# A two-layer graph network: the order of the adjacency's columns, scaling in place, x loads nine ahead in halves, and h turned before a weight

## The chip, the cores and the metric

The kernel runs on one core of a Trainium2 chip. The metric is device time in microseconds (us); that of the kernel before is the median of three runs. A core has five engines with an instruction stream each: TensorE (PE in the profile; its weight loads are PEld), VectorE (DVE), ScalarE (ACT), GpSimd (POOL) and SyncE (SP). Here SP and POOL issue the transfers (DMA). SBUF is the memory on the chip, of 128 partitions; PSUM is the one TensorE writes to; DRAM is outside.

## The reference

There are B = 16 batches of N = 1024 nodes with C = 256 channels, all in fp32. Cut to what matters:

```
# layer 0
h  = max(layernorm(x), 0)
m  = mean over channels of h                      # one number for each node
A  = |  |sigmoid(m_j - m_i) - 0.5| - 0.5 | * 2 ;  A_s = (A + A^T)/2
q  = relu((h^T @ (adj * A_s)) * para)^T           # "graph"
k, v = split(h @ kv_w)
x  = x + softmax(q k^T * scale) v                 # 4 heads of 64 channels
# layer 1
h  = max(layernorm(x), 0)
A_n   = adj + I
deg   = column sums of A_n + row sums of A_n - diagonal of A_n ;  dinv = 1/sqrt(deg)
A_hat = A_n * dinv[:, None] * dinv[None, :]
z1 = (A_hat @ h) @ W1^T + b1                      # 512 channels
z2 = relu(batchnorm(z1)) @ W2^T + b2              # 256 channels
x  = x + batchnorm(z2)
```

The two batch norms take their statistics over all batches and nodes, so the second layer can't be finished batch by batch: everything up to z1 must be there for all batches before z2 begins, and all of z2 before the end.

## The kernel before, in words

The work is written into one function, `fast_path`, with the orders of all engines written by hand (`tc.manual_schedule`): an engine runs its instructions in the order of the program text and waits where an operand isn't ready. Tile pools decide which buffer a new tile gets; a tile whose buffer is still in use waits for the last reader.

**Start.** `turn_adj` (L688) turns adj through TensorE into `ahatT`, eight groups of 128 nodes, copied out of PSUM by ACT (four) and VectorE (four) at L692. `diagonal` (L707) picks the diagonal and adds the identity on POOL, 16 instructions at L711 and L712, and VectorE sums what was picked (L713). `column_sums`, `roots`, `roots_row` (L725 copies a row out of PSUM) and `scale_adj` (L728) make A_hat out of it; the last two are laid between the matmuls of batch 1's graph. The columns of `ahatT` are the nodes in their own order.

**Stage 1, batch by batch.** For batch b the loop runs the attention of b (scores L362, exponentials on ACT, values L403), then the graph of b+1, and then linear1 of b (A_hat @ h at L551, W1 at L624; out of PSUM by L635 on VectorE and L637 on ACT), which stores z1 to DRAM; the x of layer 1 goes to DRAM too. The graph (L291) takes 64 matmuls L308, eight steps c of eight, over the weights w of c = 0 to 7. Each w is made by ACT in two instructions (L262, L265) and finished by VectorE (L266). Then follow k (L326) and v (L341), which need h with the channels on partitions. That is what `turn_h` (L271) makes: two VectorE transposes of 32x32 blocks (L278), one for each half of the channels, and 32 transfers of 32 KB (L285) on POOL's queue that put the blocks in their place (`f_hT<-f_hQ`). What stands between the matmuls of a graph is given by the dict `between` (L796): ahead of c = 0 stand w of c = 2 (`more(2)`), `turn_h`, the steps `left` of the attention that is ending, w of 3 and of 4. TensorE has no part in these steps; VectorE, ACT and POOL run them in this order.

**Stage 2.** The 32 blocks of 512 columns of z1 come back from DRAM (pool `io`, AHEAD = 7 buffers of 1 MB; `Pair.load`, `fetch_all` at L1025), batch norm and relu are applied, and z2 = W2 @ relu(...) is computed, mostly in pairs of blocks (`Pair`); z2 stays in SBUF but for the last batch, which stays in PSUM. After the last pair the first seven x of layer 1 are requested on SP (L1082, `load_x1` at L871, 1 MB in each transfer with 8 KB in a row). The last products (L1119) of four z tiles, which lie in four buffers "z" of the pool `lasting`, close the statistics.

**The end** (L1148) runs over the batches. The output's rows are dealt so that partition p holds nodes 8p to 8p+7, "(p i)". `finish` scales z2 of the next batch with the batch norm's factors, ACT the first half of the channels (L1138), VectorE the second (L1140); it reads z2 with a step of 8 elements, so that the nodes p*8+i of one i become neighbours, and writes tiles `f_zo` in the four "z" buffers. TensorE turns them, 16 transposes in each batch (L1158), into two PSUM buffers; VectorE adds each half to x (L1167); POOL stores each half, 512 KB (L1168); and SP then requests the x of batch b+7, which waits for the stores of batch b, whose buffer it takes:

```
for i0, ps in zip(range(0, NC, 4), outs):
    here = xt[:, i0 : i0 + 4, :]
    nc.vector.tensor_add(here, here, ps)
    nc.gpsimd.dma_start(out_v[:, i0 : i0 + 4, :], here)
if b + AHEAD < B:
    load_x1(b + AHEAD)
```

Of the kernel before, what the change touches and what calls it, by code (L numbers as in the profile page):

```python
# [17 lines left out]
P = 128  # L18
# [3 lines left out]

ENG = mybir.EngineType
I32 = mybir.dt.int32
AHEAD = 7
LIMIT = 1e18


# [1 line left out]
def fast_path(  # L30
# [124 lines left out]
    with ExitStack() as stage:  # L155
# [522 lines left out]
                xs[b] = load_x(b)  # L678


        ahatT = big.tile([P, NC, N], F32, tag="ahatT", name="f_ahatT")
        deg = small.tile([P, NC], F32, tag="deg", name="f_deg", bufs=1)
        rsum = small.tile([P, NC], F32, tag="rsum", name="f_rsum", bufs=1)
        diag = small.tile([P, NC], F32, tag="diag", name="f_diag", bufs=1)
# [3 lines left out]
        def turn_adj(i, copy):  # L688
            ps = ps_s.tile([P, NC, P], F32, tag="s", name=f"f_adjps_{i}")
            for m in range(NC):  # L690
                nc.tensor.transpose(ps[:, m, :], adj_t[i][:, ts(m, P)], ident)
            copy(ahatT[:, :, ts(i, P)], ps)  # L692

        def unused(name):
            return pp.tile([P, N], F32, tag="p", name=f"f_unused_{name}")
# [11 lines left out]
        def diagonal():  # L707
            on = unused("d").rearrange("p (m q) -> p m q", q=P)
            for m in range(NC):
                block = ahatT[:, m, ts(m, P)]  # L710
                nc.gpsimd.tensor_mul(on[:, m, :], block, ident)  # L711
                nc.gpsimd.tensor_add(block, block, ident)  # L712
            nc.vector.tensor_reduce(diag, on, AX.X, ALU.add)  # L713

        def roots():
# [25 lines left out]
        with tc.manual_schedule(engines={ENG.PE, ENG.Activation, ENG.DVE, ENG.Pool, ENG.SP}):  # L741
# [35 lines left out]
            for b in range(B):  # L777
# [14 lines left out]
                def more(c):  # L792
# [71 lines left out]

    with ExitStack() as stage:
        big = stage.enter_context(tc.tile_pool(name="fbig2", bufs=1))
        io = stage.enter_context(tc.tile_pool(name="fio", bufs=AHEAD))

        xts = {}

        def load_x1(b):  # L871

            xts[b] = io.tile([P, NC, C], F32, tag="x1", name=f"f_x1t_{b}")
            nc.sync.dma_start(xts[b], x1_d[b].rearrange("(p i) d -> p i d", i=NC))

        st2 = big.tile([P, CC, TT, 6], F32, tag="st2", name="f_st2")
        with tc.manual_schedule(engines={ENG.PE, ENG.Activation, ENG.DVE, ENG.Pool, ENG.SP}):
# [39 lines left out]
            class Pair:  # L917
# [5 lines left out]
                def load(self):  # L923
                    p = self.p
                    t0, t1 = self.t

                    def two(name):
                        t = io.tile([P, 2, 2, 512], F32, tag="x1", name=f"f_z{name}_{p}")
                        return t[:, 0], t[:, 1]

                    self.t2, self.t3 = two("t23")
                    one, other = two("b1")
                    self.b[0, 0] = fetch(t0, 0, one)
                    self.b[1, 0] = fetch(t0, 2)
                    self.b[0, 1] = fetch(t1, 0, other)
                    one, self.t4 = two("b2")
                    self.b[1, 1] = fetch(t1, 2, one)

                def relu(self, k, j):
                    relu_on(self.b[k, j], 2 * k)  # L940
# [114 lines left out]
            for p in SEVEN:  # L1055
                now, soon = pairs[p], pairs.get(p + 1)
                if p + 2 in pairs:
                    pairs[p + 2].load()
                now.m2()
                stats(now.t[0], 0)  # L1060
                if soon:
                    soon.relu(0, 0)
                    soon.relu(0, 1)
                now.m6()
                now.keep(0, 1)
                now.m7()
                if soon:
                    soon.relu(1, 1)
                    soon.relu(1, 0)
                now.m5()  # L1070
                now.keep(1, 1)
                if soon:
                    soon.sums13()
                    soon.m1()
                    soon.keep(0, 0)
                else:
                    for t in rest:
                        fetch_all(t)
# [43 lines left out]
                bn2.invert(c, c + 1)  # L1122
                bn2.affine(c, c + 1)


            turned_z = {}

            def finish(b, c, i0, i1):
                if i0 == 0:
                    turned_z[b, c] = lasting.tile(  # L1130
                        [P, NC, P], F32, tag="z", name=f"f_zo_{b}_{c}", bufs=4
                    )

                def scaled(out, src):
                    src = src.rearrange("p (q i) -> p i q", i=NC)[:, i0:i1, :]
                    s, t = bn2.s[:, c : c + 1], bn2.t[:, c : c + 1]
                    if c == 0:
                        nc.scalar.activation(out, src, AF.Identity, bias=t, scale=s)  # L1138
                    else:
                        nc.vector.tensor_scalar(out, src, s, t, ALU.mult, ALU.add)  # L1140

                if b + 1 < B:
                    scaled(turned_z[b, c][:, i0:i1, :], z2[:, c, b, :])
                else:
                    for g in range(NH):
                        scaled(turned_z[b, c][:, i0:i1, ts(g, P // NH)], last[g, c])

            for b in range(B):  # L1148
                xt = xts.pop(b)
# [2 lines left out]
                for i0 in range(0, NC, 4):  # L1152
                    ps = ps_out.tile([P, 4, C], F32, tag="out", name=f"f_outps_{b}_{i0}")
                    for c in range(CC):
                        if b == 0:
                            finish(b, c, i0, i0 + 4)
                        for i in range(4):
                            nc.tensor.transpose(  # L1158
                                ps[:, i, ts(c, P)], turned_z[b, c][:, i0 + i, :], ident
                            )  # L1160
                    outs.append(ps)
                if b + 1 < B:
                    for c in range(CC):
                        finish(b + 1, c, 0, NC)
                for i0, ps in zip(range(0, NC, 4), outs):
                    here = xt[:, i0 : i0 + 4, :]
                    nc.vector.tensor_add(here, here, ps)  # L1167
                    nc.gpsimd.dma_start(out_v[:, i0 : i0 + 4, :], here)  # L1168
                if b + AHEAD < B:
# [515 lines left out]
```

## Time and profile before

| | |
|---|---|
| median of three runs | 2504.25 us (2500.96 to 2507.36) |
| profiled execution | 2502.86 us, of it the span 2501.1; mean clock of TensorE 0.992 |
| moved by DMA | 263.42 MB, 105 GB/s over the span |
| DMA packets | 169239; under 2 KB 120465, under 8 KB 166545 |
| x loads of the end, f_x1t<-fx | 16 of 1 MB, 8.2 us from issue to landing (median) |
| stores of the end, out_dram<-f_x1t | 32 of 512 KB, 13.2 us |
| hT transfers, L285 | 480 on POOL (and 32 for the first batch on SP) |

The span is one execution on the chip, taken by the profiler; the table of times holds other executions of the same program, which differ by up to 0.26% from one another. A row of the profile's groups reads: line, engine, operation, result<-operands by the program's names, partitions x elements, number; busy us in all and mean ns of one; and then the idle time of that engine just ahead of these instructions, with what ended most of it. In the 40 slices a digit is the busy share in tenths. The list of waits names for each wait of an engine the instruction or transfer that ended it.

### The profile page before, as it was taken

The page shows a single profiled execution, that of the slowest core. Times are in us where ns is not written, and L with a number is a line of the kernel's source. Part 1 is how long each engine was busy: PE and PEld are TensorE (multiplying, and loading weights), DVE is VectorE, ACT ScalarE, POOL GpSimd, SP SyncE. Part 2 cuts the span into 40 slices and gives each one's busy share as a digit, 9 for nine tenths or more (in the row PEclk, how much of TensorE's full clock was granted, in tenths as well). Part 3 has the DMA queues.
Part 4 walks back from the last instruction along what each step waited for, and adds up shares of the span by engine and source line. Part 5 has one row for each costly group of instructions (what it writes and reads, how often), then busy time and mean ns, then how long its engine had stood idle before and what let it go on. Part 6 is the DMA issues. An engine that isn't in the chain of part 4 may idle for free.

```text
span 2501.1 us, 24402 instructions
## 1 busy us (share of the span) xinstructions
PE 2432.2 (97%) x8122; PEld 1074.5 (43%) x8122; DVE 1625.7 (65%) x2223; ACT 1302.0 (52%) x1854; POOL 328.1 (13%) x577
## 2 busy tenths in 40 slices
PE   7999999999999999999999999999999999999984
PEld 4443444434343434344443434343444434444443
DVE  4786667484838475665848393857667586567665
ACT  7845545454636464554536363645555456256543
POOL 2030202020110302020202002030202020000012
PEclk9999999999999999999999999999999999999997
DMA  5031414131322324141322232242424120445549
GB/s 168 7 129 59 135 59 135 59 104 53 107 84 63 115 62 132 59 135 59 118 70 87 71 94 91 59 127 59 135 60 135 59 68 29 148 172 180 212 159 355
DMA packets 169239, 263.42 MB, mean 105 GB/s; under 512 B 37009, under 2 KB 120465, under 8 KB 166545
## 3 DMA queue, kind: packets, MB, share of 16 engines
q1 hardware_dynamic: 148944, 229.23, 28.4%
q0 software_dynamic: 20160, 32.55, 4.1%
q8 instruction: 66, 1.08, 0.2%
q14 instruction: 69, 0.56, 0.1%
HBM read 157.82 MB, written 70.31 MB: 91 GB/s over the span
## 4 chain that ended last, share of the span: by engine, by line
PE 82%; DMA 7%; DVE 5%; ACT 3%; issue 1%; SPq 1%; POOL 1%; DVEq 0%; POOLq 0%; ACTq 0%
PE f_s L362 15%; PE f_o L403 15%; PE f_aps L551 15%; PE f_gps L308 13%; PE f_zps L624 8%; PE f_vps L341 4%; PE f_kps L326 4%; PE f_zx L953 3%; PE f_zm L953 2%; DMA out_dram<-f_x1t 2%; PE f_z2ps L889 2%; DVE f_acc L379 1%; DMA f_hT<-f_hQ 1%; SPq L467 1%; DMA frow<-f_sums 1%
## 5 line engine op out<-in xcount | busy, mean ns | idle before, releaser
L370 ACT ACTIVATE f_p<-f_s 128x1024 f32<-128x1024 f32 x512 | 477.3, 1046 | 145.4 <-PE f_s L362 144.0
L379 DVE TENSOR_TENSOR f_acc<-f_acc,f_p 128x1024 f32<-128x1024 f32 x384 | 470.5, 1225 | 41.1 <-DVE f_acc L379 1.4
L362 PE MATMUL f_s<-f_qT,f_kT 64*128 64x512 f32 x2048 | 458.1, 596 | 0.0
L403 PE MATMUL f_o<-f_p,f_v 128*64 128x512 f32 x2048 | 453.6, 595 | 0.0
L308 PE MATMUL f_gps<-f_w,f_h_a 128*128 128x512 f32 x1024 | 444.7, 594 | 2.2 <-DVE f_w L266 2.2
L285 POOL DMA_DIRECT2D f_hT<-f_hQ x480 | 235.7, 499 | 1226.0 <-DVE f_hQ L278 838.3
L362 PEld LDWEIGHTS f_s<-f_qT,f_kT 64*128 64x128 f32 x2048 | 189.4, 185 | 265.9 <-ACT f_p L370 121.6
L308 PEld LDWEIGHTS f_gps<-f_w,f_h_a 128*128 128x128 f32 x1024 | 192.8, 190 | 250.4 <-issue 229.3
L403 PEld LDWEIGHTS f_o<-f_p,f_v 128*64 128x64 f32 x2048 | 141.4, 137 | 304.3 <-issue 274.0
L624 PE MATMUL f_zps<-f_aggT,f_w1T 128*128 128x512 f32 x512 | 222.5, 592 | 0.0
L266 DVE SCALAR_TENSOR_TENSOR f_w<-f_w,f_adj 128x1024 f32<-128x1024 f32 x128 | 155.1, 1213 | 83.2 <-ACT f_w L265 76.2
L262 ACT ACTIVATE f_w<-f_row,f_col 128x1024 f32<-128x1024 f32 x128 | 148.2, 1158 | 52.3 <-DMA f_row<-frow 47.7
L637 ACT ACTIVATE f_z<-f_zps,f_b 128x512 f32<-128x512 f32 x98 | 62.1, 684 | 202.9 <-PE f_zps L624 202.9
L219 ACT ACTIVATE f_h_a<-f_x,f_shift_a,f_rstd_a 128x256 f32<-128x256 f32 x128 | 75.0, 587 | 175.5 <-DVE f_shift_a L214 175.5
L641 DVE BATCH_NORM_STATS2 f_st<-f_z 128x6 f32<-128x512 f32 x128 | 82.2, 684 | 124.6 <-ACT f_z L637 124.6
L219 ACT ACTIVATE f_h_b<-f_x,f_shift_b,f_rstd_b 128x256 f32<-128x256 f32 x128 | 64.6, 587 | 170.7 <-DVE f_shift_b L214 170.7
L624 PEld LDWEIGHTS f_zps<-f_aggT,f_w1T 128*128 128x128 f32 x512 | 97.2, 190 | 122.0 <-issue 122.0
L265 ACT ACTIVATE f_w<-f_w 128x1024 f32<-128x1024 f32 x128 | 135.3, 1057 | 4.1
L593 DVE TENSOR_TENSOR f_aggT<-f_u,f_aps 128x512 f32<-128x512 f32 x16 | 11.0, 688 | 180.5 <-PE f_aps L551 180.5
L326 PE MATMUL f_kps<-f_hT,f_kvw 128*128 128x512 f32 x256 | 114.6, 595 | 6.4 <-DMA f_hT<-f_hQ 5.5
L551 PE MATMUL f_aps<-f_ahatT,f_hs 128*128 128x512 f32 x256 | 115.1, 592 | 0.0
L551 PE MATMUL f_aps<-f_ahatT,f_h_b 128*128 128x512 f32 x256 | 112.9, 593 | 0.9 <-ACT f_z L637 0.9
(151 smaller groups left out, 2453.5 us busy)
## 6 DMA issues: line engine op xcount, KB each, us to landing
f_t<-ft SPq DMA_DIRECT2D x84, 512.0 KB, 8.2
f_x<-in_x_dram SPq DMA_DIRECT2D x32, 1024.0 KB, 6.0
fz<-f_z SPq DMA_DIRECT2D x64, 512.0 KB, 3.5
f_zb<-fz SPq DMA_DIRECT2D x36, 512.0 KB, 4.5
f_para<-in_L_gnn_para_dram SPq DMA_DIRECT2D x32, 512.0 KB, 4.7
f_att<-f_oT SPq DMA_DIRECT2D x512, 32.0 KB, 1.9
fx<-f_x SPq DMA_DIRECT2D x16, 1024.0 KB, 6.0
f_x1t<-fx SPq DMA_DIRECT2D x16, 1024.0 KB, 8.2
```

The source lines that it names most:

```text
L219: nc.scalar.activation(self.h[:, c, :], self.xt[:, c, :], AF.Relu, bias=self.shift[:, c : c + 1], scale=self.rstd[:, c : c + 1], accum_out ...
L262: nc.scalar.activation(w, rows[b], AF.Abs, bias=cols[b][:, c : c + 1], scale=0.5 / C)
L266: nc.vector.scalar_tensor_tensor(w, w, 1.0, adj_t[c], ALU.subtract, ALU.mult)
L285: queue.dma_start(to[ts(k, 32), ts(a, 32 * NC)], t[ts(a, 32), k].rearrange("i c r -> i (c r)"),)
L308: nc.tensor.matmul(gps[d][:, ts(g, 512)], hs[b][:, c, ts(d, P)], w[:, ts(g, 512)], start=(c == 0), stop=(c == NC - 1),)
L326: nc.tensor.matmul(ps[:, ts(g, 512)], kvw_t[:, e, ts(d, P)], hT[e][:, ts(g, 512)], start=(e == 0), stop=(e == CC - 1),)
L362: nc.tensor.matmul(ps[:, e, :], kT[rows_e, pair, ts(m, P)], qT[rows_e, pair, ts(g, 512)], start=True, stop=True,)
L370: nc.scalar.activation(p, ps, AF.Exp)
L379: nc.vector.tensor_add(acc_of[s], acc_of[s], p)
L403: nc.tensor.matmul(o_of[s][e * HD : (e + 1) * HD, :], v[:, m, ts(2 * pair + e, HD)], p[:, e, :], start=(m == 0), stop=(m == NC - 1),)
L551: nc.tensor.matmul(ps, left[:, m, :], right(m), start=(m == 0), stop=(m == KH - 1),)
L624: nc.tensor.matmul(ps[:, i, :], w1T[:, d, ts(f, P)], aggT[:, d, :], start=(d == 0), stop=(d == CC - 1),)
```

## The change

Four edits go together.

1. The columns of `ahatT` are put in the end's order: column i*128+p holds node 8p+i. `turn_adj`'s copies write runs of 16 and read PSUM at a step of 8, `diagonal`'s POOL operations go over views with a step of 8, and the row of factors is copied in the same order. So z1 and z2 come out in this order too.
2. In the end `finish` scales in place in z2, contiguously, and writes no `f_zo`; the last batch goes from PSUM into the buffers of `w2n` and `w2T`. The transposes read z2.
3. AHEAD is 9. The pool `io` holds 14 half buffers (512 KB) in place of 7 whole ones, and every load of x for the end comes as two halves of 4 KB in a row. Seven batches are requested as before; two more, 7 and 8, are requested after the last statistics' instructions in the program's text, into the four "z" buffers, which no `f_zo` needs any more. In the end batches 9 to 15 are requested, each into the half buffers of batches 0 to 6. z1's blocks of `fetch_all` come as two halves of 512 KB.
4. In `between[0]`, `turn_h(b + 1)` stands ahead of `more(2)`.

```diff
-AHEAD = 7
+AHEAD = 9
...
+        ROW = P // NC
+        def columns(i):
+            view = ahatT.rearrange("p m (i q) -> p m i q", i=NC)
+            return view[:, :, :, ROW * i : ROW * (i + 1)]
+        def as_columns(nodes):
+            return nodes.rearrange("p (q i) -> p i q", i=NC)
...
-            copy(ahatT[:, :, ts(i, P)], ps)
+            copy(columns(i), ps.rearrange("p m (q i) -> p m i q", i=NC))
...
-                block = ahatT[:, m, ts(m, P)]
-                nc.gpsimd.tensor_mul(on[:, m, :], block, ident)
-                nc.gpsimd.tensor_add(block, block, ident)
+                block = columns(m)[:, m]
+                nc.gpsimd.tensor_mul(as_columns(on[:, m, :]), block, as_columns(ident))
+                nc.gpsimd.tensor_add(block, block, as_columns(ident))
...
-            nc.scalar.copy(t, ps.rearrange("p c q -> p (c q)"))
+            nc.scalar.copy(
+                t.rearrange("p (i c q) -> p c i q", i=NC, c=NC),
+                ps.rearrange("p c (q i) -> p c i q", i=NC),
+            )
...
-                        more(2), lambda: turn_h(b + 1), left[0], left[1], left[2], more(3),
+                        lambda: turn_h(b + 1), more(2), left[0], left[1], left[2], more(3),
...
-        io = stage.enter_context(tc.tile_pool(name="fio", bufs=AHEAD))
+        io = stage.enter_context(tc.tile_pool(name="fio", bufs=NH * (AHEAD - 2)))
...
-        def load_x1(b):
-
-            xts[b] = io.tile([P, NC, C], F32, tag="x1", name=f"f_x1t_{b}")
-            nc.sync.dma_start(xts[b], x1_d[b].rearrange("(p i) d -> p i d", i=NC))
+        def load_x1(b, pool=None, tag="x1", bufs=None):
+
+            xts[b] = []
+            for h in range(NH):
+                t = (pool or io).tile([P, NC // NH, C], F32, tag=tag, name=f"f_x1t_{b}_{h}", bufs=bufs)
+                nc.sync.dma_start(t, x1_d[b].rearrange("(p h i) d -> p h i d", h=NH, p=P)[:, h])
+                xts[b].append(t)
...
-                z = io.tile([P, FC, 512], F32, tag="x1", name=f"f_zz_{t}")
-                nc.sync.dma_start(z, z1_d[t])
                 for f2 in range(0, FC, 2):
-                    zs[t, f2] = z[:, f2 : f2 + 2, :]
+                    z = io.tile([P, 2, 512], F32, tag="x1", name=f"f_zz_{t}_{f2}")
+                    zs[t, f2] = fetch(t, f2, z)
...
-                    for n in range(AHEAD):
+                    for n in range(AHEAD - 2):
                         load_x1(n)
...
+            for b in range(AHEAD - 2, AHEAD):
+                load_x1(b, lasting, "z", 4)
+            ready = {}
             def finish(b, c, i0, i1):
-                if i0 == 0:
-                    turned_z[b, c] = lasting.tile(
-                        [P, NC, P], F32, tag="z", name=f"f_zo_{b}_{c}", bufs=4
-                    )
+                s, t = bn2.s[:, c : c + 1], bn2.t[:, c : c + 1]
                 def scaled(out, src):
-                    src = src.rearrange("p (q i) -> p i q", i=NC)[:, i0:i1, :]
-                    s, t = bn2.s[:, c : c + 1], bn2.t[:, c : c + 1]
                     if c == 0:
                         nc.scalar.activation(out, src, AF.Identity, bias=t, scale=s)
                     else:
                         nc.vector.tensor_scalar(out, src, s, t, ALU.mult, ALU.add)
                 if b + 1 < B:
-                    scaled(turned_z[b, c][:, i0:i1, :], z2[:, c, b, :])
+                    ready[b, c] = z2[:, c, b, :]
+                    at = ready[b, c][:, i0 * P : i1 * P]
+                    scaled(at, at)
                 else:
+                    ready[b, c] = lasting.tile(
+                        [P, N], F32, tag=("w2n", "w2T")[c], name=f"f_zo_{c}"
+                    )
                     for g in range(NH):
-                        scaled(turned_z[b, c][:, i0:i1, ts(g, P // NH)], last[g, c])
+                        scaled(ready[b, c][:, ts(g, 512)], last[g, c])
...
-                                ps[:, i, ts(c, P)], turned_z[b, c][:, i0 + i, :], ident
+                                ps[:, i, ts(c, P)], ready[b, c][:, ts(i0 + i, P)], ident
...
-                    here = xt[:, i0 : i0 + 4, :]
+                    here = xt[i0 // 4]
```

`Pair.load` takes its buffers as half buffers too, at the same places.

More of the change, by code (lines that the diff above doesn't have):

```diff
@@ L925, in load, with new @@
                     t0, t1 = self.t
[L927 to L933, printed above, removed]
+                    def new(name):
+                        return io.tile([P, 2, 512], F32, tag="x1", name=f"f_z{name}_{p}")
+                    self.t2, self.t3 = new("t2"), new("t3")
+                    self.b[0, 0] = fetch(t0, 0, new("b11"))
                     self.b[1, 0] = fetch(t0, 2)
-                    self.b[0, 1] = fetch(t1, 0, other)
-                    one, self.t4 = two("b2")
-                    self.b[1, 1] = fetch(t1, 2, one)
+                    self.b[0, 1] = fetch(t1, 0, new("b12"))
+                    self.b[1, 1] = fetch(t1, 2, new("b22"))
+                    self.t4 = new("t4")
                 def relu(self, k, j):
@@ L1123, in fast_path @@
                 bn2.affine(c, c + 1)
-            turned_z = {}
+            for b in range(AHEAD - 2, AHEAD):
+                load_x1(b, lasting, "z", 4)
+            ready = {}
             def finish(b, c, i0, i1):
-                if i0 == 0:
-                    turned_z[b, c] = lasting.tile(
-                        [P, NC, P], F32, tag="z", name=f"f_zo_{b}_{c}", bufs=4
-                    )
+                s, t = bn2.s[:, c : c + 1], bn2.t[:, c : c + 1]
                 def scaled(out, src):
-                    src = src.rearrange("p (q i) -> p i q", i=NC)[:, i0:i1, :]
-                    s, t = bn2.s[:, c : c + 1], bn2.t[:, c : c + 1]
                     if c == 0:
```

## The prediction, made before the changed kernel ran

> **What bounds the kernel now.** I read the page's busy shares first, then the slices, TensorE's waits, and at last the end by windows and timeline.
>
> ```profile
> PE 2432.2 (97%) x8122; PEld 1074.5 (43%) x8122; DVE 1625.7 (65%) x2223; ACT 1302.0 (52%) x1854; POOL 328.1 (13%) x577
> PE   7999999999999999999999999999999999999984
> DMA  5031414131322324141322232242424120445549
> PE 82%; DMA 7%; DVE 5%; ACT 3%; issue 1%; SPq 1%; POOL 1%; DVEq 0%; POOLq 0%; ACTq 0%
> ```
>
> TensorE is busy 97% of the span, and 9 tenths in every slice but the first and the last two. The change removes no matmul, so all it can win is in TensorE's waits and in the two ends of the span. The waits:
>
> ```profile
> PE f_outps L1158 <- DVE f_x1t L1167: 21.2, 14, 4.3
> PE f_adjps L691 <- DMA f_adj<-in_adj_dram: 8.5, 1, 8.5
> PE f_kps L326 <- DMA f_hT<-f_hQ: 5.5, 7, 1.6
> PE f_gps L308 <- DVE f_w L266: 2.2, 2, 1.3
> ```
>
> (us in all, times, longest.) Two of them are touched: 5.5 us in which the kv product waits for the turned h (seven waits in 15 graphs), and the end (L1158), where the 21.2 us say only that TensorE is idle behind something slower. What that is, the windows tell (us, then PE, PEld, DVE, ACT, POOL busy, clock, DMA share, GB/s):
>
> ```profile
> 2412.00:2424.00 12.00, 7.55 (x29) 4.37 (x28) 7.90 (x17) 6.51 (x4) 0.88 (x2) 0.89 0.00 0
> 2424.00:2444.00 20.00, 14.28 (x96) 12.03 (x94) 19.56 (x18) 12.72 (x7) 9.10 (x12) 0.90 0.87 290
> 2444.00:2464.00 20.00, 11.87 (x86) 9.80 (x87) 19.00 (x18) 12.62 (x6) 6.10 (x9) 0.96 1.02 410
> 2464.00:2484.00 20.00, 11.58 (x60) 10.18 (x58) 11.96 (x12) 3.70 (x3) 4.69 (x9) 0.70 1.02 400
> 2484.00:2497.00 13.00, 0.00 (x0) 0.00 (x0) 0.94 (x1) 0.00 (x0) 1.53 (x3) 0.58 0.83 335
> ```
>
> Three stages: 12 us with no transfer at all (last products, statistics, first scalings); 20 us in which VectorE is full (19.56 of 20) and DMA moves 290 GB/s; then 53 us of full DMA at 400 to 410 GB/s, the last 12 of them after the last addition. Rate times length over the last four windows is 5.8 + 8.2 + 8.0 + 4.4 = 26.4 MB, and nine loads and sixteen stores of 1 MiB are 26.2: the end is a fixed number of bytes through a full pipe, which starts at the first store (2424.2 on POOL's timeline). The pipe has a dead stretch just ahead of it.
>
> [...] loads (SP) and stores (POOL) together stay at 400 to 410 GB/s, so each MiB of load in the last 73 us is taken from the stores. [...] L1140 takes 1238 ns for 1024 elements, reading at a step of 8. [...] ACT's activation with a pointer takes 2264 ns at step 8 (L1138) and 1158 ns contiguously (L262).
>
> ```profile
> L1138 ACT ACTIVATE f_zo<-f_z,f_bn_t,f_bn_s 128x1024 f32<-128x1024 f32 x14 | 31.7, 2264 | 20.8 <-PE f_outps L1158 20.8
> L1140 DVE TENSOR_SCALAR f_zo<-f_z,f_bn_s,f_bn_t 128x1024 f32<-128x1024 f32 x14 | 17.3, 1238 | 0.0
> ```
>
> **Part 1, nine batches ahead.** Two loads (2 MiB, 2.10 MB) leave the full pipe and land in the dead stretch. At 410 GB/s they were 5.1 us. In their new place they wait for the four "z" buffers of the last z products, which come free one by one between about 2411 and 2416.6 (the last statistics read at 2416.6 follows the last product), and need 5 to 8 us: done by some 2424, before additions 7 and 8 by far. SP issues them behind the earlier x1 loads, and nothing else stands behind them on SP but loads that wait for stores. Gain 5.1. Against it, the seven loads left have 4-KB packets and not 8-KB ones: in the trace's packet records a 4-KB store packet takes 159 ns and an 8-KB load packet 309, 26 and 27 bytes per ns; 3% of the 7.3 MB (18 us) is 0.5 us. Net -4.6, between -2 (small packets beside stores cost more) and -5.1.
>
> **Part 2, scaling in place and contiguous.** VectorE has two additions (1.14 each, start to start) and one scaling (1.14) in each batch: 3.41 us per MiB, 307 GB/s, which is what the 290 of the first window is. The scaling without its step is not in the trace. [...] It counts only until the first load joins, 2424.2 to 2438.1[...]. As the stores lag production already (250 GB/s in its first half, POOL's own issue taking 0.53 to 0.98), I take half: -1.0 (0 to -1.9). The first store comes earlier by the two half-size scalings [...] and the full one [...] that stand on VectorE around the first addition: about -0.6 (-0.3 to -0.9). ACT's 2264 falls to about 1158, at no gain: VectorE has no idle time at L1140 and L1167 that ACT ended. Scaling in place also drops ACT's wait for free f_zo buffers; it was 20.8 us of idleness of an engine off the path. End in all: -4.6 - 1.0 - 0.6 = -6.2 (-2.5 to -8).
>
> **Part 3, h turned ahead of w2.** In each graph VectorE now runs the two L278 (2.36 us) before w2's L266 (1.18), so all 32 hT transfers of POOL can start 1.18 earlier. The graph with the longest wait:
>
> ```profile
> 402.49 2.36 DVE L278 STREAM_TRANSPOSE f_hQ<-f_h_a 128x1024 f32<-128x1024 f32 x2
> 404.36 3.98 POOL L285 DMA_DIRECT2D f_hT<-f_hQ  x8 [83.20 <-DVE f_hQ L278]
> 412.41 3.91 POOL L285 DMA_DIRECT2D f_hT<-f_hQ  x8 [4.08 <-DMA f_hT<-f_hQ]
> 430.96 4.53 PE L326 MATMUL f_kps<-f_hT,f_kvw 128*128 128x512 f32 x10 [1.63 <-DMA f_hT<-f_hQ]
> ```
>
> POOL issues eight, then waits for the landing of the first eight, and so on in four rounds, so a later round moves by what the landings move by. Were the whole 1.18 passed on, the seven waits (1.63, 0.32, 0.45 and 1.39 in one graph, 0.34, 0.65, 0.67) would fall to 0.45 in one graph and 0.66 in another: -4.3. Were the landings set by the 3 MB of f_t loads around them, nothing. I take -2.5. The other side: w2's L266 ends 2.36 later, at about 5.4 us after the graph's first matmul; TensorE needs it at c = 2, 6.9 after (3.46 per c). Slack 1.5 (1.0 in the tightest graph), so the cost is nothing while that cover lasts. Queued behind on VectorE: L475 and w3's L266, whose place is unchanged, as the three instructions together last as long.
>
> **Part 4, columns in the end's order.** Once, at the start: eight copies L692 (1.0 us on ACT, 1.2 on VectorE) read PSUM at step 8 and write runs of 16, sixteen POOL operations L711 and L712 (0.455 each) go over step-8 views, one row copy is permuted. PSUM at step 8 is in the trace: L1140 from f_z2ps 804 ns and L1138 772, for 128x512, against 746 and 684 for L635 and L637, contiguous; that is 8 to 13%, so 0.1 per copy. [...] POOL ends at 60.75, VectorE reduces to 61.9 and has nothing due before 73.92: 12 us of cover hide it. Taken at +0.2 (0 to +3, should the copies double as ACT's read of SBUF did).
>
> **Sum.** -6.2 - 2.5 + 0.2 = -8.5. Against the profiled execution (2502.86; span 2501.1) 2494.4; that one is 1.4 under the median, so 2495.8.
>
> **Rivals.** (A) As above: 2495.8, own range 2492 to 2500, chance 0.58.
> (B) More: all 4.3 of part 3, and the end loses 9, since loads per half also start earlier and the pipe is full sooner: -13, 2491. For it: 110 GB/s are missing in 20 us, 2.3 MB or 5.7 us. Against: POOL's 0.98-us issues and slow first landings (9.05 us) limit that stage too. Chance 0.16.
> (C) The bytes don't show: two loads less, but a mix of small packets, or stores alone, at a lower rate (335 GB/s in the last window), eats it. Then -0.6 - 2.5 + 0.2: 2501.3. Against: the last window holds the pipe's running out, not a slower pipe. Chance 0.14.
> (D) The start's strided copies and POOL lie open, +6: 2501.8. Against: 12 us of cover. Chance 0.05.
> (E) Slower: w2. VectorE reaches L266 more than 1.5 us later than worked out, because L278 stretches beside POOL's issues or L278 waits for its hQ buffers; from there each us costs every one of 15 graphs. One us beyond gives +15: 2511. For it: two graphs already wait for a w (2.2 us). Against: L278 follows VectorE's own work without a gap in the trace. Chance 0.07.
>
> **How the numbers follow.** A measurement of this kernel can tell about 0.3%, 7.5 us, from no change: below 2496.7 is faster. A lies 0.9 below that with some 4 either way, so 0.35 of its 0.58, and all of B: faster 0.51. The rest of A, C and D: same 0.42. E: slower 0.07. The range leaves out E and the far half of B: 2489 to 2503.
>
> **What would show it.** Part 1: 2 MB at over 250 GB/s between 2410 and 2424, seven x1 loads after the first store, and the last packet five us sooner after the first store. Part 2: L1140 at 0.6 to 0.75 us, L1138 near 1.16, the first full window above 310 GB/s. Part 3: the hT wait at 1 to 4 us; a growing L308 wait on L266 speaks for E. Part 4: L711 at up to 0.7, TensorE's work before 75 us at the same times. The prediction is wrong if the pipe's length follows the stores alone, or if the kv product's wait stays at 5.5.

## The result, and the profile after

The changed kernel took 2494.07 us (median of eight runs, 2490.89 to 2499.59), the kernel before 2501.07 in eight runs: a ratio of 0.9971, 95% interval 0.9958 to 0.9984, so 7.0 us less. Run again beside other kernels (E5 below) the ratio was 0.9960 (0.9946 to 0.9973), 9.1 us less. The forecast was 8.5 less (2495.8 us, counted from the earlier median of 2504.25). The sum was good; its terms, as the experiments show, were not: the end gave about 8.3 us where 6.2 were forecast, and the turned h gave nothing that the medians show where 2.5 were forecast.

Read the profile of after in the same order. The page's busy shares and slices:

```profile
PE 2425.7 (97%) x8122; PEld 1067.2 (43%) x8122; DVE 1619.0 (65%) x2223; ACT 1285.2 (52%) x1854; POOL 326.1 (13%) x577
DMA  5041414231322414141313223242413211354559
```

TensorE still rules the span. Its waits in after:

```profile
PE f_outps L1172 <- DVE f_x1t L1181: 11.8, 13, 1.6
PE f_adjps L701 <- DMA f_adj<-in_adj_dram: 8.7, 2, 8.2
PE f_gps L308 <- DVE f_w L266: 2.8, 2, 1.9
PE f_kps L326 <- DMA f_hT<-f_hQ: 1.4, 2, 1.1
```

At first sight the wait for hT fell from 5.5 to 1.4, just what part 3 hoped for. It is the trap of this case: one execution of a wait that changes from execution to execution. The end by windows:

```profile
2408.00:2420.00 12.00, 7.73 (x32) 4.16 (x30) 7.86 (x21) 10.12 (x10) 1.10 (x2) 1.00 0.55 175
2420.00:2440.00 20.00, 14.68 (x112) 11.70 (x110) 20.00 (x21) 8.58 (x9) 7.68 (x14) 1.00 0.92 333
2440.00:2460.00 20.00, 14.23 (x108) 11.53 (x109) 20.00 (x21) 0.00 (x0) 4.65 (x9) 1.00 1.03 418
2460.00:2472.00 12.00, 2.82 (x23) 2.17 (x21) 5.69 (x6) 0.00 (x0) 3.68 (x7) 0.78 1.03 417
2472.00:2485.00 13.00, 0.00 (x0) 0.00 (x0) 0.00 (x0) 0.00 (x0) 1.60 (x3) 0.50 0.80 325
```

The dead stretch now moves 175 GB/s for 12 us, 2.1 MB: the two loads. The first full window has 333 GB/s in place of 290, and the full pipe 417 in place of 400 to 410. The group of the stores in before, and the groups of the scaling and of the stores in after:

```profile
L1168 POOL DMA_DIRECT2D out_dram<-f_x1t x32 | 21.4, 670 | 46.8 <-DVE f_x1t L1167 26.0 <-issue 11.8 <-DMA out_dram<-f_x1t 9.0
```

```profile
L1147 ACT ACTIVATE f_z<-f_z,f_bn_t,f_bn_s 128x1024 f32<-128x1024 f32 x14 | 16.0, 1227 | 0.0
L1149 DVE TENSOR_SCALAR f_z<-f_z,f_bn_s,f_bn_t 128x1024 f32<-128x1024 f32 x14 | 11.3, 809 | 0.0
L1182 POOL DMA_DIRECT2D out_dram<-f_x1t x32 | 17.6, 551 | 41.6 <-DVE f_x1t L1181 24.6 <-DMA out_dram<-f_x1t 14.8 <-DVE f_z L1149 1.9
```

ACT's scaling fell from 2264 to 1227 ns, VectorE's from 1238 to 809, and POOL's issue of a store, which took 670 ns on average before, to 551. The last goes with the scaling: in the records of each kernel nine of these issues begin beside a scaling of VectorE, and they end 0.12 to 0.13 us after it, but for two in after, which end 0.21 and 0.26 after it and took 0.53 us. In before seven of the nine took 0.95 to 0.98 us, and in after, where the scaling ends sooner, six took 0.55 to 0.60. Nearly all other issues took 0.53 us.

**The two profiles differ by more than the medians**, 12.0 us in span. Part of that is chance, and can be placed. The clock that TensorE was granted was 0.50 from 18.37 to 21.79 us in before and from 19.25 to 29.49 in after, so the first products of a graph, from 23.3 us on, ran at half the clock in after alone; the same eight matmuls in before, and then in after:

```profile
23.36 3.70 PE L308 MATMUL f_gps<-f_w,f_h_a 128*128 128x512 f32 x8 [1.33 <-DVE f_w L266]
```

```profile
23.33 6.75 PE L308 MATMUL f_gps<-f_w,f_h_a 128*128 128x512 f32 x8 [1.87 <-DVE f_w L266]
```

That cost after 3 us, of which it was 1.8 behind by the second batch's graph. It made good 4.8 between there and the last products, mostly by hT waits that happened to be short, and 8.9 from the last products to the end of the span. So the experiments below are judged by two things: the medians, good to some 2 to 3 us, and the length of the end itself, from the end of the last product to the end of the last packet, worked out from the records of each trace. In five profiles of the changed kernel's end it repeats within 0.4 us (70.0 to 70.4), and so tells apart what the medians can't. The end of the kernel before scatters more, 77.6 to 79.3 in four profiles, so a difference from it is good to about 1 us.

### The profile page after: what moved, and what is told of

Read it like the earlier page. It is cut to its first block, busy times and chain, and to the rows that moved or that the text cites. A ratio compares the mean times of both kernels' runs of the same rounds, so it can differ in the third digit from the quotient of the medians.

```text
span 2489.1 us, 24427 instructions
## 1 busy us (share of the span) xinstructions
PE 2425.7 (97%) x8122; PEld 1067.2 (43%) x8122; DVE 1619.0 (65%) x2223; ACT 1285.2 (52%) x1854; POOL 326.1 (13%) x577
```

## The experiments

Each kernel ran beside the kernel before on the same chip; the ratio is to that, with its 95% interval.

| | edit | median, us | of before, us | ratio |
|---|---|---|---|---|
| E1 | before + turned h first | 2500.42 | 2500.07 | 1.0002 (0.9994 to 1.0011) |
| E2 | after, w2 first again | 2490.28 | 2500.07 | 0.9964 (0.9951 to 0.9978) |
| E3 | after, seven ahead | 2496.51 | 2500.07 | 0.9985 (0.9979 to 0.9992) |
| E4 | before + columns | 2500.10 | 2500.07 | 1.0001 (0.9993 to 1.0009) |
| E5 | after again | 2492.21 | 2501.26 | 0.9960 (0.9946 to 0.9973) |
| E6 | after + f_t loads late | 2484.14 | 2501.26 | 0.9929 (0.9916 to 0.9943) |
| E7 | after + scaling on ACT | 2491.54 | 2501.26 | 0.9960 (0.9946 to 0.9973) |
| E8 | after + w2 2.4 us later | 2505.90 | 2501.26 | 1.0021 (1.0014 to 1.0028) |
| E9 | after, whole loads | 2491.91 | 2502.18 | 0.9954 (0.9940 to 0.9968) |
| E10 | before + f_t loads late | 2493.89 | 2502.18 | 0.9963 (0.9950 to 0.9977) |
| E11 | after + two store queues | 2489.09 | 2502.18 | 0.9947 (0.9933 to 0.9961) |
| E12 | E6 and E11 | 2484.73 | 2502.18 | 0.9925 (0.9911 to 0.9939) |

### The edits apart: E1 to E4

**E1, the turned h alone.**

```diff
-                        more(2), lambda: turn_h(b + 1), left[0], left[1], left[2], more(3),
+                        lambda: turn_h(b + 1), more(2), left[0], left[1], left[2], more(3),
```

> The kernel before, with h turned ahead of w2 and nothing else. Theory 1 (the turned h's earlier start is worth what the two traces show): the kv product's wait on the hT transfers falls from 5.5 to about 1.4 us, and the time by about 4 us, 2 to 5. Theory 2 (the landings of the hT transfers vary from execution to execution and the lower wait in the trace of after is chance): the wait stays between 3 and 7 us and the time within 1 us of before. Both: the first full window of the end stays at about 290 GB/s, and the wait on w2 does not grow.

1.0002: nothing, and by the interval at most 1.5 us of gain. The waits of E1:

```profile
PE f_kps L326 <- DMA f_hT<-f_hQ: 6.4, 5, 1.6
PE f_gps L308 <- DVE f_w L266: 3.8, 2, 2.9
```

The wait for hT is 6.4, higher than before's 5.5, and the two waits for w are those at the start: theory 2. Where the earlier start is lost is seen best in the graph whose wait is the longest in E1. POOL's timeline in before, where this graph's first matmul starts at 1079.76:

```profile
1085.55 3.98 POOL L285 DMA_DIRECT2D f_hT<-f_hQ  x8 [84.24 <-DVE f_hQ L278]
1092.81 4.04 POOL L285 DMA_DIRECT2D f_hT<-f_hQ  x8 [3.28 <-DMA f_hT<-f_hQ]
1097.90 1.47 POOL L285 DMA_DIRECT2D f_hT<-f_hQ  x3 [1.05 <-DVE f_st_b L204]
```

and in E1, where it starts at 1079.33:

```profile
1083.80 3.98 POOL L285 DMA_DIRECT2D f_hT<-f_hQ  x8 [82.33 <-DMA f_t<-ft]
1091.75 0.99 POOL L285 DMA_DIRECT2D f_hT<-f_hQ  x2 [3.97 <-DMA f_hT<-f_hQ]
1092.92 2.98 POOL L285 DMA_DIRECT2D f_hT<-f_hQ  x6 [0.19 <-issue]
1098.02 1.47 POOL L285 DMA_DIRECT2D f_hT<-f_hQ  x3 [2.12 <-DVE f_mv_b L206]
```

The first eight go out at 4.5 us after the graph's first matmul and not at 5.8, the second round begins at 12.4 and not 13.1, the third at 18.7 and not 18.1. In the mean of the thirteen graphs that load f_t: first issue at 5.4 in before and 4.0 in E1, second round 11.9 and 11.6, last issue 24.9 and 25.0. Of 1.4 us, 0.3 outlive the first landing, and at the third round (16.9 and 17.1) nothing is left.

**E2, everything but the turned h.** Its diff is E1's, taken back in the changed kernel.

> The changed kernel with w2 ahead of the turned h again, so all of the end's and the columns' edits without that of the turned h. Theory 1: slower than the changed kernel by about 4 us, with hT waits of 4 to 6 us, and faster than before by 4 to 6; in the trace the time from the first store to the last packet is 60 to 62 us, against 72.6 before. Theory 2: as fast as the changed kernel, 7 us under before, since the end has all of the gain.

0.9964, with an hT wait of 4.2 us; E5, the same kernel with the turned h, gives 0.9960. Theory 2's size is right: within what the medians tell, the end has all of the gain. The length of its end is 70.2 us, as the changed kernel's, where the kernel before has 79.3. E1, E4 and E10, whose end is the same as before's, have 78.7, 77.6 and 78.4; the mean of the four is 78.5.

**E3, seven ahead.**

```diff
-AHEAD = 9
+AHEAD = 7
...
-        io = stage.enter_context(tc.tile_pool(name="fio", bufs=NH * (AHEAD - 2)))
+        io = stage.enter_context(tc.tile_pool(name="fio", bufs=NH * AHEAD))
...
-                    for n in range(AHEAD - 2):
+                    for n in range(AHEAD):
                         load_x1(n)
...
-            for b in range(AHEAD - 2, AHEAD):
-                load_x1(b, lasting, "z", 4)
```

> The changed kernel with seven batches loaded ahead in place of nine: no load into the z buffers, nine loads beside the stores in the end. Scaling in place, columns, halves and the turned h stay. Theory 1 (the end is a fixed number of bytes through a full pipe): 2.1 MB at about 415 GB/s, so the time from the first store to the last packet is 5 us longer than in the changed kernel, and the time 5 us more. Rival (the end is set by how fast VectorE and POOL bring stores, and the loads fit beside them): 0 to 2 us more.

Its ratio lies 0.0025 above E5's and 0.0014 above the changed kernel's first, 3.5 to 6 us. The end is 75.1 us long, 4.9 more than with nine ahead; 5 were expected from the bytes. Its windows:

```profile
2405.00:2417.00 12.00, 8.61 (x29) 5.15 (x28) 7.84 (x20) 9.84 (x10) 1.10 (x2) 0.90 0.00 1
2417.00:2437.00 20.00, 14.76 (x110) 11.93 (x109) 19.51 (x21) 8.86 (x9) 7.20 (x14) 0.98 0.89 328
2437.00:2457.00 20.00, 13.23 (x88) 10.51 (x85) 16.76 (x17) 0.00 (x0) 4.73 (x9) 0.88 1.03 417
2457.00:2477.00 20.00, 10.65 (x48) 8.54 (x48) 10.63 (x11) 0.00 (x0) 5.31 (x10) 0.59 1.03 418
```

The dead stretch is back (1 GB/s in 12 us), and the full pipe lasts longer at the same 417 GB/s: a fixed number of bytes through a full pipe, whatever else VectorE has time for (it is free for 3 of 20 and then 9 of 20 us). The other theory falls. What E3 keeps against before, 78.5 to 75.1, is 3.4 us (2.5 to 4.2 by the single profiles). I put it down to the scaling, and what follows from it for POOL's issues. The half loads differ too; E9 tests them, though with nine batches ahead.

**E4, the columns alone.** The edits of the first part of the diff (`columns`, `as_columns`, the copies and the diagonal), with before's end.

> The kernel before with the columns of ahatT in the end's order and the end as it was, so the rows of the output's second part are permuted; all times are those of the same amount of work. Theory: POOL's sixteen operations go from 0.455 to about 0.52 us and nothing else moves: within 1 us of before. Rival: TensorE's first scores start later by 2 us or more, since the strided copies and POOL's operations hold it up, and the time is 2 us more.

1.0001, so within 2.3 us of nothing: the slower start of the prediction's rival D isn't there. In the changed kernel itself POOL's group reads

```profile
L721 POOL TENSOR_TENSOR f_unused_d<-f_ahatT,f_ident 128x128 f32<-128x128 f32 x8 | 4.2, 527 | 10.4 <-ACT f_unused_r L708 10.4
```

527 ns for 455, so 16% more, below the 0.7 us that the prediction allowed; the copies out of PSUM at a step of 8 are unchanged (1008 ns for 1004 on ACT, 1218 for 1221 on VectorE). TensorE's first scores do start 1.8 us later in the profile of after. That is the half clock of the first eight matmuls, 6.75 us in after and 6.76 in E4; E2, with the same strided copies, has them in 3.70, and is 0.8 us ahead of before by the second graph.

### Where the turned h's head start goes: E5, E6, E10

**E5, the changed kernel again.** No edit.

> The changed kernel once more, on one chip with the three kernels after it. The kernel with the turned h's edit undone came out at 0.9964 of before and the changed kernel at 0.9971, on different occasions. Theory 1 (the turned h ahead of w2 is worth nothing, and costs nothing): the ratio to before is 0.996 to 0.998, and the wait of the kv product for hT lies anywhere between 1.4 and 6.4 us, as in the profiles so far. Theory 2 (it costs something): the ratio stays above 0.997.

Ratio 0.9960 and an hT wait of 5.6 us. So one and the same kernel shows 1.4 us in one execution and 5.6 in another. Of all profiles with the f_t loads at their old place, eight have the turned h first and waits of 1.1 to 6.4 us, 3.4 in the mean; three have w2 first, 4.2 to 5.5, 4.7 in the mean. (The lowest, 1.1, is E8's, whose k product comes later.) This is theory 1 as far as the runs can tell: a gain of about 1 us is within that scatter and within E1's interval; one of 2.5 is outside E1's interval.

**E6, the f_t loads late.** If the landing of the first eight hT transfers holds the rest, what holds the landing? Six loads of f_t, 3 MB, which SP requests at the graph's start and linear1 first reads some 48 us later (400.4 and 448.7 in before). In E6 they are requested at step c = 6:

```diff
                     if 0 < b < B - 2:
-                        thirds = load_thirds(b)
+                        between[6].insert(0, lambda: got.update(t=load_thirds(b)))
+                    got = {}
                     qkv = graph(b + 1, between)
+                    thirds = got.get("t")
```

> The changed kernel with the six f_t loads (3 MB, SP) requested at step c = 6 of the graph, after the hT transfers, and not at its start. Theory (the landings of the first eight hT transfers are set by the f_t loads beside them, so that an earlier start of the turned h is lost at the first landing): POOL's four rounds run one after the other in all graphs as they do in the first and the last, where no f_t is loaded, the last hT is issued about 19 to 20 us after the graph's first matmul in place of 22 to 30, the wait for hT falls to nearly 0 and the time by 2 to 5 us. Rival (the rounds are set by the hT transfers' own small packets or by the exchange of the attention's output on SP): rounds and waits stay. If f_t then comes too late, linear1 waits for it, up to 7 us in each of 13 graphs.

0.9929, 8.1 us under E5, more than expected, and TensorE's list of waits has no line for hT at all. POOL's timeline in the graph whose wait the prediction showed:

```profile
402.26 15.73 POOL L285 DMA_DIRECT2D f_hT<-f_hQ  x32 [81.49 <-DVE f_hQ L278]
```

and SP's:

```profile
391.49 27.27 SPq L467 DMA_DIRECT2D f_att<-f_oT  x26
418.86 1.00 SPq L303 DMA_DIRECT2D f_para<-in_L_gnn_para_dram  x2
419.95 3.22 SPq L530 DMA_DIRECT2D f_t<-ft  x6
```

All 32 go out in one stretch of 15.7 us, where before needed 21.5 with its stops. The median time of an hT transfer from issue to landing, in E6 (396 to 416 us) and then in before (399 to 416 us), beside f_t:

```profile
f_hT<-f_hQ POOLq DMA_DIRECT2D x28, 32.0 KB, 1.7
```

```profile
f_hT<-f_hQ POOLq DMA_DIRECT2D x16, 32.0 KB, 6.1
```

The rival that blamed the small packets themselves, or the attention's output on SP, falls: both are still there in E6. The hT transfers share the pipe with the f_t loads, as the stores of the end share it with the loads of x. In before DMA moves 292 GB/s from 404 to 408 us and 352 from 408 to 412, at a busy share of 0.93 and 1.01; the first eight hT transfers, issued from 404.36 on, land at 412.1 to 415.1, and the six f_t loads, issued from 400.37 on, at 404.3 to 416.1. The prediction reckoned with such sharing at the end; here I did not apply it to the full. The delay then meets a second group of loads. The last eight hT transfers of before, issued at 421.9 to 425.4, run beside two of f_para (1 MB, issued from 421.90 on) and take 2.9 to 5.2 us each; in E6 all 32 are issued before f_para is requested. Moving f_para alone was not tried.

**E10, the same edit on the kernel before**, with w2 first.

> The kernel before with the six f_t loads requested at step c = 6 of the graph and nothing else: w2 still ahead of the turned h. Theory (the f_t loads alone set the landings): the wait for hT falls from 5.5 to 0 us, the second round of eight hT transfers begins about 9 us after the graph's first matmul in place of 11.9, the last is issued at about 21 us in place of 24.9, and the time falls by 5 to 8 us. Rival (it needs the turned h ahead of w2 as well): a wait of 2 us or more stays, and the time falls by less than 4 us.

0.9963 (8.3 us), no hT wait left. The same graph in E10:

```profile
405.62 15.68 POOL L285 DMA_DIRECT2D f_hT<-f_hQ  x32 [83.13 <-DVE f_hQ L278]
```

The second round begins 9.3 us after the first matmul in the mean, the last is issued at 21.0. So with the f_t loads out of the way the turned h needs no head start: the k product wants hT at 27.6. The order of `between` was not what set the wait. How long the k product took over its 7.03 us, added over the graphs, bears it out: 7.3 us in before, 8.8 in E1, 3.0 in after, 6.8 in E5, 0.0 in E6, E10 and E12. The length of the stretch from the second batch's graph to the last product goes by that sum: it is 2281.0, 2281.4 and 2281.5 us in E6, E10 and E12, and in every other profile but E8's it is longer by the sum, to within 1 us (2289.5 in before, 2284.7 in after, 2287.6 in E5).

### The slack of w2: E8

```diff
+        def late():
+            for _ in range(2):
+                nc.vector.scalar_tensor_tensor(
+                    adj_t[2], adj_t[2], 1.0, adj_t[2], ALU.mult, ALU.max
+                )
...
-                        lambda: turn_h(b + 1), more(2), left[0], left[1], left[2], more(3),
+                        lambda: turn_h(b + 1), late, more(2), left[0], left[1], left[2], more(3),
```

> The changed kernel with two more VectorE instructions of 1.2 us, which copy adj onto itself, between the turned h and w2 in each graph, so w2 is 2.4 us later still. Theory (w2 has 1.5 us of slack left in the changed kernel, worked out from the trace of before): TensorE waits for w2 about 0.9 us in each of 15 graphs, L308's wait on L266 grows by 10 to 16 us and the time by as much. Rival (the slack is larger, or what VectorE has queued behind it takes the loss up): less than 4 us. If the slack were less than worked out: over 20 us.

2505.90, 13.7 us over E5; 15 graphs by 0.9 us would be 13.5. TensorE's wait in E8:

```profile
PE f_gps L314 <- DVE f_w L266: 15.0, 17, 1.6
```

Fifteen graphs wait now, besides the two waits at the start that every profile has. TensorE's matmuls of c = 2 start 0.9 us later in most graphs, up to 1.5 in one. The slack of 1.5 us that the prediction worked out from the timeline of before was there to a few tenths, so the turned h's edit is free, and rival E's mechanism is real and begins where it was said to. That the two totals agree so well is in part luck. The k product starts 1.1 us later or more in each graph, 18.1 in all; some 5 come back, since it then finds more of hT landed (what it takes over its 7.03 us falls from 6.8 in E5 to 1.7).

### What else holds the end: E7, E9, E11, E12

**E7, the scaling on ACT.**

```diff
-                    if c == 0:
+                    if c == 0 or b > 0:
                         nc.scalar.activation(out, src, AF.Identity, bias=t, scale=s)
```

> The changed kernel with both halves of the end's scaling on ACT but for the first batch; VectorE only adds. VectorE's period per batch falls from 2.98 to about 2.3 us and the first store comes 0.7 us sooner. Theory 1 (while the pipe is not yet full, the end is bound by how fast stores are produced): the first 20 us of the end move 370 to 410 GB/s in place of 333, and the time falls by 2 to 4 us. Rival (POOL's issue and its wait for the first landing, or the bytes alone, set the end): the same window stays at 330 to 345 and the time falls by less than 1 us.

The same ratio as E5, and an end of 69.4 us, 0.8 less; the first 20 us after the first store move 347 GB/s and not 338. The rival holds: in the changed kernel VectorE's production is no longer what keeps the pipe from filling. The first store comes 0.3 us sooner after the last product (6.4 and 6.75), a part of the gain.

**E9, whole loads.** The buffers, `load_x1`, `Pair.load` and `fetch_all` as in the kernel before, but for batches 7 and 8:

```diff
-        io = stage.enter_context(tc.tile_pool(name="fio", bufs=NH * (AHEAD - 2)))
+        io = stage.enter_context(tc.tile_pool(name="fio", bufs=AHEAD - 2))
...
+            if pool is None:
+                t = io.tile([P, NC, C], F32, tag="x1", name=f"f_x1t_{b}")
+                nc.sync.dma_start(t, x1_d[b].rearrange("(p i) d -> p i d", i=NC))
+                xts[b] = [t[:, 0:4, :], t[:, 4:8, :]]
+                return
```

> The changed kernel with the x loads of the end, but for batches 7 and 8, and z1's blocks as whole 1-MB transfers with 8 KB in a row, in the seven whole buffers of the kernel before. Theory 1 (halves cost 0.5 us by their smaller packets and gain as much by coming free earlier): 70.2 us from the last product to the last packet as in the changed kernel, within 0.7 us; so all of the 3.4 us that the end gains without the two extra batches is the contiguous scaling's. Theory 2 (a good part of the 3.4 us is the halves'): 72 us or more, the first load after the first store later than 4.2 us.

The end is 70.1 us long, as in the changed kernel: theory 1. With nine ahead, halves neither cost nor gain; the first load comes 0.4 us later after the first store (4.6 and 4.2), and it doesn't matter.

**E11, two queues for the stores.** In every kernel so far POOL stops after its fifth store of the end. POOL's timeline in before:

```profile
2431.17 0.53 POOL L1168 DMA_DIRECT2D out_dram<-f_x1t  x1 [1.31 <-DVE f_x1t L1167]
2435.23 2.50 POOL L1168 DMA_DIRECT2D out_dram<-f_x1t  x3 [3.53 <-DVE f_x1t L1167]
```

and in after:

```profile
2425.87 0.53 POOL L1182 DMA_DIRECT2D out_dram<-f_x1t  x1 [1.31 <-DVE f_x1t L1181]
2429.93 1.65 POOL L1182 DMA_DIRECT2D out_dram<-f_x1t  x3 [3.53 <-DVE f_x1t L1181]
```

The releaser named, VectorE's addition, had long ended, as the three stores issued at once tell. E11 gives each second half to ACT's queue:

```diff
+                if b == 0:
+                    for soon in (1, 2):
+                        finish(soon, 0, 0, NC)
+                if b + 3 < B:
+                    finish(b + 3, 0, 0, NC)
                 if b + 1 < B:
-                    for c in range(CC):
-                        finish(b + 1, c, 0, NC)
+                    finish(b + 1, 1, 0, NC)
...
-                    nc.gpsimd.dma_start(out_v[:, i0 : i0 + 4, :], here)
+                    queue = nc.scalar if i0 else nc.gpsimd
+                    queue.dma_start(out_v[:, i0 : i0 + 4, :], here)
```

> The changed kernel with the second half of each batch's stores issued on ACT's queue in place of POOL's, and ACT's scalings three batches ahead so that a store waiting for VectorE's addition does not hold them. Theory (in the first 20 us of the end POOL stops at the sixth store until the first has landed, 3.5 us, and that keeps the pipe at 336 GB/s): without the stop the first 20 us move over 380 GB/s and the time falls by 2 to 3 us. Rival (production or the pipe itself): the same window stays within 330 to 350 and the time within 1 us of the changed kernel.

0.9947. The pipe reaches 402 GB/s in the third stretch of 4 us after the first store, where the changed kernel has 323; over the first 20 us it moves 365 and not 338, between what the theory and the rival named. Yet the last packet comes 68.8 us after the last product, only 1.5 sooner. From the last product to the end of the span it is 71.5 us and not 75.5: the other 2.6 lie behind the last packet, where the span runs on for 5.3 us in the changed kernel, all of whose last stores are POOL's, and for 2.7 in E11, where ACT's come last. The records show what runs there: a closing DRAIN of POOL, 2.84 us long, which begins 1.6 us behind the last packet in the changed kernel; in E11 it is over before ACT's last store has landed. By the medians E11 gains 3 us on E5's ratio, and their intervals overlap. The reason that I gave is not shown: POOL in E11 stops again after five stores, though these now come half as often:

```profile
2430.65 0.53 POOL L1187 DMA_DIRECT2D out_dram<-f_x1t  x1 [2.46 <-DVE f_x1t L1185]
2436.57 1.05 POOL L1187 DMA_DIRECT2D out_dram<-f_x1t  x2 [5.38 <-DVE f_x1t L1185]
```

A wait for the first store's landing would not last 3.53 us to the hundredth in before, after and E7, nor come at the sixth store here, 17 us after the first. It seems to go by the number of POOL's stores. What it is stays open.

**E12, both.** The diffs of E6 and E11.

> The changed kernel with both: the f_t loads at step c = 6 and the stores on two queues. Theory: the gains add up, 5 to 8 us by the f_t loads and 0 to 3 by the queues, so 2482 to 2486 us where the kernel before takes 2501.

2484.73, ratio 0.9925 (0.9911 to 0.9939), beside E6's 0.9929. The f_t loads' gain is there; whether the queues add to it the medians can't tell. The end of its span comes 73.1 us after the last product, between E11's 71.5 and E6's 75.3; its last packet comes at 70.3, no sooner than E6's at 70.0, so what the queues gain here lies behind the last packet. E6 and E12 are both faster than the kernel before by 0.7%, and clear of the changed kernel by their intervals.

## Why the prediction was right, and where it wasn't

- **What bounds the kernel, and the end as bytes through a full pipe:** right. Taking the two loads back in E3 makes the end 4.9 us longer and leaves the rate at 417 GB/s; rival C, in which the bytes don't show, falls.
- **Part 1:** -4.6 forecast, -4.9 measured (75.1 to 70.2). The term that was off is the +0.5 for 4-KB packets: E9 has whole loads and the same end. The 12-us window of the two loads shows 175 GB/s and not the 250 named as a sign, which cost nothing: in after the last of them landed at 2419.08, before the first store at 2420.27.
- **Part 2:** -1.6 forecast (the "half" of 1.9, and 0.6 for the first store), -3.4 measured (78.5 to 75.1, or 2.5 to 4.2 by the scatter of before's end). The first store comes 0.75 sooner after the last product (7.62 to 6.87), near the 0.6. The term that was mis-sized is production: taken at half of its bound, 1.0, for fear of stores that lag; from the first store to the last packet E3 takes 68.2 us where before's end takes 70.9 in the mean, 2.7 less. The first 20 us went from between 295 and 310 GB/s to 341: 0.6 to 0.9 MB, or 1.5 to 2.2 us; the rest is a pipe fuller by about 2% later on. That the bound was 1.9 is luck. It rests on a length of the scaling without its step that was my estimate and that the trace of before does not show, and on a wrong reading: 2438.1 is the issue of the second load after the first store. The first was issued at 2428.75 and its first packet ran at 2429.8, 5.6 us after the first store and not 13.9, so the same estimate would have given 0.8 us. The gain did not stop when a load joined. It came with a scaling of 0.81 us, above the 0.6 to 0.75 that the prediction named as the sign by the same estimate: the step had cost VectorE only a third of its time (1238 ns with it, 809 without). Whether POOL's shorter issues (670 to 551 ns) are what let all of it through was not tried apart.
- **Part 3:** -2.5 forecast, 0 measured, 1.5 at most (E1, 1.0002; E2 beside E5). The prediction's own sign of being wrong, a wait that stays at 5.5, was met in E1 (6.4) and E5 (5.6). The failing step is "so a later round moves by what the landings move by ... I take -2.5": the landings hardly moved, as f_t's 3 MB set them (E6, E10), which the prediction had as its other bound. A choice in the middle between two bounds was made where the timeline could have decided: the first and the last graph, which load no f_t, run through without a stop in before too.
- **w2's slack of 1.5 us:** right (E8), and with it the cost of nothing for that side.
- **Part 4:** +0.2 forecast, nothing measurable (E4). POOL's operations take 16% more, and the 12 us of cover hide it, as said.
- **The sum:** -8.5 forecast; by the experiments -8.3 for the end and 0 for the turned h and for the columns, -7.0 and -9.1 by the two sets of medians. Two errors, 2.1 us too little in the end and 2.5 too much in part 3, made it look better than it was. Rival B named the larger end (9), and had it for the reason that the pipe fills sooner, but with 4.3 of part 3 that never came. (Its 110 GB/s over 20 us are 2.2 MB, not 2.3.)

## What to carry to other kernels

Before a transfer is started earlier, ask what its landing waits for: if it shares the pipe with megabytes that nobody needs yet, move these, and not the transfer (an hT transfer took 6.1 us beside the f_t loads and 1.7 without them). The wait for hT, which differed from graph to graph, also differed from run to run; one profile before and one after can show such a wait shrink by chance, so undo the edit alone. And where an end is limited by bytes, count them: moving 2 MiB into a stretch in which nothing is transferred was worth its length at the full rate, to some tenths (4.9 us measured, 5.0 by 417 GB/s).

## What the runs showed of the hardware that was not expected

- POOL's issue of 512-KB stores stops after the fifth for 3.53 us, the same in all twelve profiles here whose stores are all POOL's, and after five of POOL's own in E11 and E12, there for 5.38 us where the other gaps are about 2.5. The cause is open.
- POOL's issues of stores that began beside a scaling of VectorE ended 0.12 to 0.13 us after the scaling, all nine in before and seven of nine in after. Those that began beside an addition alone took 0.53 us, but for the first store's (0.61) and the first behind the stop in before (1.45).
- Reading PSUM at a step of 8 (with writes in runs of 16) cost the copies out of PSUM nothing (1004 and 1008, 1221 and 1218 ns), whereas the same step in SBUF nearly doubled ACT's activation (2264 and 1227) and cost VectorE half as much again (1238 and 809).
- TensorE's granted clock fell to 0.50 near the start for 3.4 us (before) to 10.2 (after) by the clock records of the profiles, and differs between executions of like kernels; the same eight matmuls take 3.70 or up to 6.76 us by it, which moves a profile by up to 3 us.
